# Two-layer graph kernel on one core: the second feed-forward product as seven half-size block products, and a written order for every engine

## The chip, the cores and the metric

The kernel runs on one core of a Trainium2 chip. A core has five engines that run side by side, each with its own instruction queue: TensorE (PE in the profile; its weight loads are listed as PEld), VectorE (DVE), ScalarE (ACT), GpSimd (POOL) and SyncE (SP), which issues the DMAs here. PE reads its operands from the on-chip memory SBUF and writes into the accumulator memory PSUM, which is used in tiles of one bank (128 rows by 512 float32). The metric is the time of one execution in microseconds (us). Before the change the median of three runs is 2792.41 us (2792.07 to 2793.43).

## The reference, cut to what matters

There are 128 graphs of 128 nodes with 256 features, and a 0/1 matrix of edges. Two layers follow each other. The first is a graph-attention layer with a ReLU feed-forward, the second a relational attention with eight heads and a GELU feed-forward. All is float32.

```
# layer 0
h = gat(gat(x, adj, W1, a1), adj, W2, a2)
h = layernorm(x + h)
x = layernorm(h + relu(h @ w_ff1 + b_ff1) @ w_ff2 + b_ff2)
# layer 1
attn = softmax(q @ k.T / sqrt(32));  out = sum over r of (attn * (adj == r)) @ (x @ Wv[r])
x = layernorm(x + out @ Wo + bo)
x = layernorm(x + gelu(x @ W1 + b1) @ W2 + b2)
```

In both feed-forwards the first product takes 256 features to 1024, and the second takes 1024 to 256. The second one is what this change is about.

## The kernel before

The graphs are worked on in 32 groups of four, so a group is 512 tokens (4 x 128). A group passes through five stages: load, gat (two graph-attention steps), ff0 (first feed-forward), att (relational attention) and ff1 (second feed-forward). Each stage is a Python generator that emits instructions and yields a waiting time after each step. `run` is a timetable: it takes the generator whose next time is smallest, lets it emit one step, and puts it back at its time plus the wait. In the main part a group starts every 100 units of the timetable, so that stages of five or six groups interleave. In this order PE and SP are chained by dependencies; the order of DVE, ACT and POOL is left to the scheduler of the framework.

A prefix (function `graph_layers`) loads weights, folds the gains and offsets of the normalisations into the following weights, takes three groups through gat and one through ff0, and scans the whole edge matrix for values above 1. If there are none, as here, the program takes its binary arm, in which only two of the four relations occur; else it takes a general arm. In the first and the last group (`alone`) turned features come from PE transposes (L284); in the others they go out through DRAM and back: DVE turns blocks of 32x32 (L290), SP stores them (zd) and reads them back turned (T, eT).

`feed_forward` (L323) works in two halves.

- First product, already as seven products of blocks (Winograd's form of Strassen's method) in each of two units. A unit owns two 128-row chunks of the lower and two of the upper half of the 1024 hidden features. `moving_sums` forms sums of the token blocks on POOL (L317 to L320), `weight_sums` forms those of the weights once, in the prefix. A unit has four visits, in which `product` (L341) writes into PSUM tiles `chain`, `side` and `p`: three tiles per unit, of seven in the pool `mm`. ACT copies `chain` out between its uses (L347, L354, L359) and `side` (L348), DVE adds (L355, L356), POOL adds the two upper parts (L360), ACT applies the function (L362, L368). The visits alternate between the units.
- Second product, in the plain form. `second` (L386) multiplies, for each of four token blocks, eight chunks fT (128 features by 128 tokens, the stationary operand) with wout (128 by 256, the moving operand): 32 matmuls of 256 columns. Two PSUM tiles hold the result, DVE adds it to the tokens (L396), then `normalised` follows: statistics on DVE (L258, L259), four small steps on POOL (L261 to L265), scaling on ACT (L267). `affine` (L273, POOL) applies gain and offset to the residual.

Other lines that the text below names: L186 folds offsets into wv (chunks of 512 columns), L194 does so for other weights with one moving column; L444, L452, L463 are the products of the gat stage, L478 and L483 those for q and k, L499 the scores (four row groups of 32 side by side), L550 the values, L565 the weighted sum (four column groups), L592 the output product; L512, L514, L515 are the softmax on ACT, DVE and POOL. L408 and L284 are transposes on PE.

Of the kernel before, what the change touches and what calls it, by code (L numbers as in the profile page):

```python
# [24 lines left out]
P = 128  # L25
G = 4
Q = 32
LEAD = 3
FIRST = 1
SCANS = 8  # L30
# [3 lines left out]
    "ff first half": 10, "ff half": 5, "row": 13, "gat": 22, "wh": 5.5,  # L34
# [8 lines left out]
    binary=False, times=TIMES, together=1, period=560, bufs=dict(T=3, tok=2, m=4, mm=6, v=1),  # L43
    begin=dict(load=-97, gat=-61, ff0=48, att=132, ff1=400), early={},
    kept={PE: 0, SP: 0},
# [3 lines left out]
    binary=True, together=2, period=100, bufs=dict(T=5, tok=5, m=2, mm=7, v=2),  # L49
    times=dict(TIMES, **{  # L50
        "sums": 6, "ff visits": (2.5, 2.5, 4, 4, 3.25, 3.25, 3.25, 3.25), "ff first half": 6,
        "ff half": 4, "row": 14.5, "wh": 3.5, "mask": 8.5, "av": 14.5, "wo": 12, "turned": 11,
        "next put": 2.5, "row put": 8, "affine": 13, "store": 21,
    }),
    begin=dict(load=-96, gat=-61, ff0=47, att=129, ff1=303),
    early={
        (-2, "ff1"): -43, (-1, "load"): 5, (0, "att"): -5, (-1, "ff1"): 12, (-2, "att"): -6,
        (-3, "att"): 2, (3, "ff0"): 2, (-4, "ff1"): 5, (4, "ff0"): 2,
    },
    kept={PE: 120, SP: 0},  # L60
)

PREFIX = dict(TIMES, **{
    "sums": 0.5, "ff visits": (1, 1, 2, 1, 0.5, 1, 1, 1), "ff2": 11, "ff first half": 0.5,
    "ff half": 2, "row": 6, "gat": 12.5, "wh": 4.0, "put": 0.5, "lead ff0": 3.5, "scan": 7.5,
    "scans": 25, "gats": (0, 12, 24), "fold": 24.5, "ffs": (48,), "second fold": 31.5,
})
# [16 lines left out]
class Pools:  # L84

    def __init__(self, ctx, tc, bufs):
# [3 lines left out]
        self.ps = ctx.enter_context(tc.tile_pool(name="ps", bufs=bufs["mm"], space=PSUM))  # L90
        self.dr = ctx.enter_context(tc.tile_pool(name="dr", bufs=3, space=bass.MemoryType.DRAM))
# [3 lines left out]
def constants(tc, a, c, cst, tmp, ps):  # L95
# [67 lines left out]

    def others():

        c.wq = wload("wq")
        c.wk = wload("wk")
        c.wv = wload("wv")
        c.bv = cst.tile([P, R * D], F32, name="bv")
        nc.sync.dma_start(c.bv, on_all_rows(11, R))  # L170
        c.wo = wload("wo")
        c.w1 = wload("w1")
        c.w2 = wload("w2")
# [43 lines left out]

def per_row(v, n):

    return v[:, :, None].to_broadcast([P, v.shape[-1], n])  # L220


def stages_of(tc, a, out, c, pools, plan):
# [14 lines left out]
    TB, KB = plan["bufs"]["T"], plan["bufs"]["tok"]  # L238
# [13 lines left out]
    def normalised(y, first=0, n=G):  # L252
# [565 lines left out]
```

## Time and profile before

| | before |
|---|---|
| median of 3 runs | 2792.41 us |
| profiled execution | 2792.19 us, its span 2790.4 us |
| busy PE / weight load | 2714.0 / 2148.0 us |
| busy DVE / ACT / POOL | 1507.7 / 1675.7 / 1569.2 us |
| second product L386, both layers | 913 us, 4096 passes |
| first product L341, all forms | 900 us |
| PE idle from 0 to 156 us | 28 us |
| PE idle from 2700 us to the end | 21 us |
| steady group | 83.3 us |

The profile is one execution, so its parts are to be set against that execution's own time. A group line gives line, engine, operation, written tile <- read tiles, shape and count; then busy time, mean length of one in ns, and the idle time just before with the engine that ended it. A float32 matmul appears as two passes, each with a weight load. In timeline lines the first number is the start and the second the length, both in us; x says how many equal instructions were merged. The length of a matmul includes its way through the array, so the pace of a stream is read from the distance between starts.

### The profile page before, as it was taken

What the parts mean: (1) busy time and instruction counts of PE and PEld (TensorE: products, weight loads), DVE (VectorE), ACT (ScalarE), POOL (GpSimd) and SP (SyncE); (2) the same over time, 40 slices, a digit from 0 to 9 for tenths busy, and PEclk for the clock granted to TensorE, in tenths of its full rate; (3) what the DMA queues carried; (4) which work ended last, traced back from release to release, by engine and by line L of the source; (5) the groups of instructions that cost most, each with busy time, mean ns of one, the idle gap of its engine ahead of it and who ended that gap; (6) DMA issues with size and microseconds to landing.
All of it is one profiled execution on the core that took longest, in us unless ns stands there. A gap on an engine that the chain in (4) does not pass through costs nothing.

```text
span 2790.4 us, 46726 instructions
## 1 busy us (share of the span) xinstructions
PE 2714.0 (97%) x16618; PEld 2148.0 (77%) x16618; DVE 1507.7 (54%) x2882; ACT 1675.7 (60%) x5067; POOL 1569.2 (56%) x1613
## 2 busy tenths in 40 slices
PE   7889999999999999999999999999999999999988
PEld 5667787777788777788777778777778777777767
DVE  5544565555565555565555555555556555556442
ACT  4445565666565666576565666565666566666444
POOL 2334565655665655575565565565566565566453
PEclk8999999999999999999999999999999999999989
DMA  8134555655645655655655655655554565564320
GB/s 304 32 80 96 119 115 122 128 114 123 132 111 114 139 106 119 142 109 109 141 115 112 138 112 113 132 119 113 132 118 112 127 128 112 125 134 91 90 54 16
DMA packets 1136394, 324.04 MB, mean 116 GB/s; under 512 B 886296, under 2 KB 1105944, under 8 KB 1135000
## 3 DMA queue, kind: packets, MB, share of 16 engines
q1 hardware_dynamic: 1136152, 320.96, 51.6%
q8 instruction: 134, 2.20, 0.3%
q14 instruction: 108, 0.88, 0.1%
HBM read 193.35 MB, written 127.52 MB: 115 GB/s over the span
## 4 chain that ended last, share of the span: by engine, by line
PE 73%; ACT 9%; DVE 8%; POOL 6%; issue 3%; DMA 1%; SPq 0%; ACTq 0%; DVEq 0%; POOLq 0%
PE mm L386 31%; PE mm L341 17%; PE mm L550 5%; PE av L565 4%; PE mm L478 4%; PE mm L483 4%; ACT fT L362 2%; PE mm L499 2%; ACT tok L267 2%; PE mm L452 2%; POOL e L515 2%; PE mm L592 2%; DVE nm L503 2%; POOL tok L273 2%; DVE st L258 2%
## 5 line engine op out<-in xcount | busy, mean ns | idle before, releaser
L273 POOL TENSOR_TENSOR tok<-tok,ln_rows 128x512 f32<-128x512 f32 x460 | 624.9, 1375 | 11.8 <-DVE T L290 3.5
L386 PE MATMUL mm<-w,fT 128*128 128x256 f32 x2048 | 465.1, 383 | 0.0
L386 PE MATMUL mm<-wf,fT 128*128 128x256 f32 x2048 | 448.2, 379 | 0.0
L386 PEld LDWEIGHTS mm<-w,fT 128*128 128x128 f32 x2048 | 385.3, 190 | 60.1 <-issue 6.5
L386 PEld LDWEIGHTS mm<-wf,fT 128*128 128x128 f32 x2048 | 389.4, 190 | 53.5 <-ACT fT L368 0.3
L512 ACT ACTIVATE e<-mm,nm 128x128 f32<-128x128 f32 x1024 | 358.4, 401 | 39.7 <-DVE nm L503 35.8
L515 POOL TENSOR_TENSOR e<-e,s 128x1024 f32<-128x1024 f32 x128 | 241.8, 1896 | 246.5 <-DVE s L514 131.8
L317 POOL TENSOR_TENSOR t<-T 128x256 f32<-128x256 f32 x64 | 53.9, 842 | 537.2 <-DMA T<-zd 534.5
L534 DVE TENSOR_TENSOR m<-eT,am 128x1024 f32<-128x1024 f32 x128 | 175.7, 1375 | 332.2 <-DMA eT<-zd 331.9
L267 ACT ACTIVATE tok<-tok,nmr,rstd 128x256 f32<-128x256 f32 x464 | 242.8, 610 | 165.0 <-POOL nmr L265 150.2
L512 ACT ACTIVATION_READ_ACCUMULATOR e<-mm,nm 128x1 f32 x1024 | 247.5, 242 | 0.0
L550 PE MATMUL mm<-wv,T 128*128 128x512 f32 x512 | 234.4, 601 | 0.0
L419 ACT ACTIVATE e<-e,wh 128x128 f32<-128x128 f32 x232 | 74.1, 390 | 228.9 <-DMA e<-zsd 228.9
L360 POOL TENSOR_TENSOR fT<-fT 128x512 f32<-128x512 f32 x128 | 162.1, 1276 | 67.2 <-ACT fT L359 67.2
L341 PE MATMUL mm<-T,w 128*128 128x256 f32 x768 | 192.3, 379 | 1.2 <-ACT fT L354 1.2
L341 PE MATMUL mm<-T,wf 128*128 128x256 f32 x768 | 192.7, 379 | 0.0
L362 ACT ACTIVATE fT<-fT,col 128x512 f32<-128x512 f32 x256 | 170.9, 717 | 26.9 <-DVE fT L356 26.5
L503 DVE TENSOR_REDUCE nm<-mm 128x4 f32<-128x512 f32 x256 | 163.6, 681 | 30.9 <-PE mm L499 30.9
L396 DVE TENSOR_TENSOR tok<-tok,mm 128x512 f32<-128x512 f32 x116 | 79.1, 682 | 177.6 <-PE mm L386 173.8
L258 DVE BATCH_NORM_STATS2 st<-tok 128x6 f32<-128x256 f32 x464 | 173.2, 411 | 3.0
L433 POOL TENSOR_TENSOR e<-e,s 128x512 f32<-128x512 f32 (+1 forms) x70 | 68.0, 972 | 188.9 <-DVE s L432 188.8
L550 PEld LDWEIGHTS mm<-wv,T 128*128 128x128 f32 x512 | 98.9, 194 | 97.7 <-issue 87.1
(141 smaller groups left out, 5198.3 us busy)
## 6 DMA issues: line engine op xcount, KB each, us to landing
zd<-e SPq DMA_DIRECT2D x480, 128.0 KB, 3.5
eT<-zd SPq DMA_DIRECT2D x120, 512.0 KB, 5.2
zd<-T SPq DMA_DIRECT2D x364, 128.0 KB, 3.3
T<-zd SPq DMA_DIRECT2D x91, 512.0 KB, 4.7
xt<-in_xT_dram SPq DMA_DIRECT2D x32, 512.0 KB, 6.4
e<-zsd SPq DMA_DIRECT2D x58, 256.0 KB, 5.7
tok<-in_x_dram SPq DMA_DIRECT2D x29, 512.0 KB, 5.0
out_dram<-tok SPq DMA_DIRECT2D x28, 512.0 KB, 4.7
```

What stands on the lines that cost most here:

```text
L258: nc.vector.bn_stats(st, y[:, b])
L267: nc.scalar.activation(y[:, b], y[:, b], AF.Identity, bias=nmr[:, b:b + 1], scale=rstd[:, b:b + 1])
L273: engine.tensor_tensor(y[:, b:b + n], y[:, b:b + n], v[:, None, :].to_broadcast([P, n, D]), op)
L341: nc.tensor.matmul(p[:, i], win[k][:, ts(f0 + i, P)], hs[k], start=first and i == 0, stop=True, skip_group_check=True)
L360: nc.gpsimd.tensor_add(hi[:, :, 1], hi[:, :, 1], hi[:, :, 0])
L362: nc.scalar.activation(lo[:, i], lo[:, i], func, bias=bin_[:, f0 + i:f0 + i + 1])
L386: nc.tensor.matmul(ys[b // 2][:, b % 2], fT[f][:, ts(b, N)], wout[:, f], start=b % 2 == 0 and n == 0, stop=n == FC - 1, skip_group_check=True)
L503: nc.vector.tensor_reduce(nm.rearrange("p j i -> p (j i)"), p.rearrange("p j i n -> p (j i) n"), AX.X, OP.max, negate=True)
L512: nc.scalar.activation(e[:, k], p[:, j, i], AF.Exp, bias=nms[q][:, j, i:i + 1], accum_out=s[:, k:k + 1])
L515: nc.gpsimd.tensor_mul(e, e, per_row(s, N))
L534: nc.vector.tensor_tensor(m, eT, at[:, b][:, None, :].to_broadcast([P, H, N]), OP.mult)
L550: nc.tensor.matmul(p, hT[:, b, f], wv[:, f, r:r + 2], start=f == 0, stop=f == DC - 1)
```

## The change

- The second product becomes seven products of blocks too. The hidden features are split in lower and upper half, the tokens in two pairs of graphs, the output columns in two halves of 128. `second_sums` forms differences of the weights once in the prefix (four subtractions on DVE for each layer). In each feed-forward `summed` forms, per unit, two sums on DVE and one difference on POOL, and a second POOL subtraction follows when product 2 has read its operand. Each of the seven products is 8 matmuls of 128 moving columns. Two PSUM tiles hold four half-bank results (`chain`, `last`, `side`, `other`), which DVE adds to the tokens in eight additions of 128x256.
- The first product's visits are cut differently: 1 and 2, then 6 and 5, then 7 and 3, then 4, with two PSUM tiles per unit instead of three. In the binary arm the units are visited in the order 0, 0, 1, 0, 1, 0, 1, 1.
- `run` chains every engine. Each step has waits of its own (`steps`, and lists in the prefix), and a table of lags gives every DVE, ACT and POOL instruction of a step a place in its engine's queue: time of the step plus lag.
- Token buffers are five fixed tiles used in turn, where there were three fixed and five in a pool. The statistics tiles of the normalisations have a name per place. The load of xT moves from 96 to 166.75 units before the group's time. The edge scan has 16 pieces in place of 8, into five buffers and two token tiles. Only two relations of wv are loaded and folded in the prefix; the general arm loads the others itself.

The core of the diff:

```diff
-    begin=dict(load=-96, gat=-61, ff0=47, att=129, ff1=303),
+    begin=dict(load=-166.75, gat=-56.45, ff0=40.85, att=130.4, ff1=296.05),
...
+def second_sums(nc, c, w, name):
+    k, half = w.shape[1] // 2, w.shape[2] // 2
+    b11, b12, b21, b22 = w[:, :k, :half], w[:, :k, half:], w[:, k:, :half], w[:, k:, half:]
+    t1, t2, t4 = c.second[name]
+    nc.vector.tensor_sub(t1, b12, b11)
+    nc.vector.tensor_sub(t2, b22, t1)
+    nc.vector.tensor_sub(t4, b21, t2)
+    nc.vector.tensor_sub(b12, b22, b12)
+    return None, b11, b21, b22, t4, t1, t2, b12
...
             product(chain, 1, True)
+            product(side, 2, True)
+            nc.scalar.copy(lo[:, :, 0], chain)
+            nc.vector.tensor_add(lo[:, :, 0], lo[:, :, 0], side)
+            yield
+            product(chain, 6)
             product(side, 5, True)
-            nc.scalar.copy(lo[:, :, 0], chain)
+            nc.scalar.copy(lo[:, :, 1], chain)
             nc.scalar.copy(hi[:, :, 0], side)
             yield
-            p = ps.tile([P, 2, T // 2], F32, name="mm")
-            product(chain, 6)
-            product(p, 2, True)
+            product(chain, 7)
             product(side, 3)
...
+        def summed(u):
+            lo, hi = halves[u]
+            a11, a12, a21, a22 = lo[:, :, 0], hi[:, :, 0], lo[:, :, 1], hi[:, :, 1]
+            s1, s2 = (wk.tile([P, 2, T // 2], F32, name=f"sum{i}") for i in (1, 2))
+            nc.vector.tensor_add(s1, a21, a22)
+            nc.vector.tensor_sub(s2, s1, a11)
+            nc.gpsimd.tensor_sub(a21, a11, a21)
+            return None, a11, a12, a12, a22, s1, s2, a21
...
-                nc.tensor.matmul(ys[b // 2][:, b % 2], fT[f][:, ts(b, N)], wout[:, f],
-                                 start=b % 2 == 0 and n == 0, stop=n == FC - 1, skip_group_check=True)
...
+        first, second = (ps.tile([P, 2, 2, D // 2], F32, name="mm") for _ in range(2))
+        chain, last, side, other = first[:, 0], first[:, 1], second[:, 0], second[:, 1]
+        low, high = (y[:, h:h + 2].rearrange("p b (n d) -> p n b d", n=2) for h in (0, 2))
...
+                        nc.tensor.matmul(p[:, j], parts[u][k][:, i, ts(j, N)], wout[k][:, 2 * u + i],
+                                         start=id(bank) not in done, stop=True, skip_group_check=True)
...
+        parts = [summed(0)]
+        for p, k in (chain, 1), (other, 2), (last, 4):
+            product(p, k, (0,))
+        nc.gpsimd.tensor_sub(parts[0][3], parts[0][3], parts[0][6])
+        yield TIMES["ff first half"]
+        parts.append(summed(1))
+        yield TIMES["ff sums"]
+        product(other, 2, (1,))
+        add(low[:, 0], other)
+        product(chain, 1, (1,))
+        product(last, 4, (1,))
+        nc.gpsimd.tensor_sub(parts[1][3], parts[1][3], parts[1][6])
+        add(low[:, 0], chain)
+        add(high[:, 0], last)
+        yield TIMES["ff 56"]
+        product(side, 5, (0, 1))
+        product(chain, 6, (0, 1))
+        add(high[:, 1], side)
+        add(low[:, 1], chain)
+        yield TIMES["ff 37"]
+        product(side, 3, (0, 1))
+        product(chain, 7, (0, 1))
+        add(low[:, 1], side)
...
+            y = c.y[g % TOKENS]
...
+            if lag is not None:
+                queues.setdefault(i.engine, []).append((t + lag, len(queues.get(i.engine, ())), i))
...
+    for queue in queues.values():
+        queue.sort(key=lambda x: x[:2])
+        for (_, _, first), (_, _, i) in zip(queue, queue[1:]):
+            after(i, first)
```

In the changed kernel's own line numbers, which the prediction uses where it speaks of its queues: L653 is the first product, L659, L664 and L669 ACT's copies of `chain`, L665 that of `side`, L671 POOL's addition of the upper parts, L675 and L679 the function, L687 and L688 the two sums, L689, L720 and L728 POOL's subtractions, L710 the second product, L715 the additions to the tokens, L586 the affine step, L845 the scores, L909 the weighted sum.

## Prediction

> **What bounds the kernel now.** I read first the page's shares of the span, then its 40 slices, then the chain that ended last: each says whether one engine is the end of everything.
>
> ```profile
> PE 2714.0 (97%) x16618; PEld 2148.0 (77%) x16618; DVE 1507.7 (54%) x2882; ACT 1675.7 (60%) x5067; POOL 1569.2 (56%) x1613
> PE   7889999999999999999999999999999999999988
> PEclk8999999999999999999999999999999999999989
> PE 73%; ACT 9%; DVE 8%; POOL 6%; issue 3%; DMA 1%; SPq 0%; ACTq 0%; DVEq 0%; POOLq 0%
> ```
>
> TensorE is busy 97% of the span, at full clock but in the first and last slices. The next view is a table of stretches. One group of four graphs takes 83.3 us: the same instruction (L341, t by w) starts at 1500.23 and at 1583.52. Columns: length, then busy time of PE, weight load, DVE, ACT, POOL, each with its instructions, then clock and DMA.
>
> ```profile
> 1500.20:1583.50 83.30, 82.77 (x512) 65.82 (x513) 46.88 (x88) 52.26 (x159) 49.33 (x51) 1.00 0.56 121
> ```
>
> In the steady part PE idles 0.5 us of 83.3, and no other engine passes 52.3. So time is TensorE time, and what shortens it must shorten PE's own stream. The groups of instructions (columns: form, count, busy, mean ns) say how much of that stream the change touches:
>
> ```profile
> L386 PE MATMUL mm<-w,fT 128*128 128x256 f32 x2048 | 465.1, 383 | 0.0
> L386 PE MATMUL mm<-wf,fT 128*128 128x256 f32 x2048 | 448.2, 379 | 0.0
> L386 PEld LDWEIGHTS mm<-w,fT 128*128 128x128 f32 x2048 | 385.3, 190 | 60.1 <-issue 6.5
> ```
>
> The second product is 913 us, a third of PE. A float32 matmul is recorded as two passes, each with its own weight load, so the 32 matmuls of one feed-forward are 64 passes. The mean of 379 is a latency. The pace is the distance between starts, and the timeline (start, length, instructions) gives it:
>
> ```profile
> 1545.08 13.98 PE L386 MATMUL mm<-wf,fT 128*128 128x256 f32 x64
> 1558.99 0.43 PE L565 MATMUL av<-eT,v 128*32 128x128 f32 x8
> ...
> 129.72 1.91 PE L284 MATMUL mm<-ident,e 128*128 128x128 f32 x16
> 131.46 1.89 PE L341 MATMUL mm<-T,wf 128*128 128x256 f32 x8
> ...
> 77.14 3.63 PE L194 MATMUL mm<-col,w 128*128 128x1 f32 x32
> 80.63 1.93 PE L463 MATMUL mm<-wh,e 128*128 128x256 f32 x5
> ...
> 1508.99 1.17 PE L499 MATMUL mm<-kT,T 32*128 32x128 f32 x32
> 1510.09 7.17 PE L386 MATMUL mm<-w,fT 128*128 128x256 f32 x32
> ```
>
> One block of 64 passes takes 13.91 us, 217 ns a pass. In the second layer the same work stands in three blocks (7.11 + 3.56 + 3.45 = 14.12 us). I take the mean, 14.0 us for each feed-forward, 64 of them.
>
> **The change, part by part.**
>
> *Seven products of half size.* Each product is 256 tokens by 512 by 128, so 8 matmuls with 128 moving columns; seven are 56 matmuls, 112 passes instead of 64. What is streamed falls from 64 x 256 to 112 x 128 columns, by an eighth, but the weight loads grow by three quarters. All hangs on the pace of a 128-column pass whose weights are new each time; before has no such row. The nearest rows bound it. The 16 transposes (128 columns, new weights, load 141 ns instead of 190) pace 1.74 / 16 = 109 ns. L194 (one column, full 190 ns loads) paces 3.49 / 32 = 109 ns: so a stream of full loads alone needs no more than that. L499 has both, 186 ns loads and 128 columns, but in four row groups side by side: 1.10 / 32 x 4 = 137 ns with the switch of shape included. The range is 109 to 137 ns. I take 109: the load row and the column row give it separately, and a 217 ns pass hides its 190 ns load today. Then 112 x 0.109 = 12.2, and 0.1 for the switches of shape, 12.3 us. Saved: 1.7 x 64 = **-109 us**. At 137 ns it is 15.4 + 0.1, so +96 us; from 125 ns (14.0 / 112) the change loses.
>
> The Trainium skill, "TensorE: Matmul & The Clock Gate", section "Back-to-back issue gap", speaks against this: in a stream of weight load and matmul pairs it gives about 81 ns for 128 columns where columns alone give 56, because the load is part of the spacing. If our 109 grew in that ratio, an estimate from that page, a pass would take 158 ns, a feed-forward 17.7 us, and about 235 us would be added where I count 109 saved. The two rows of 109 ns speak otherwise, but neither has full loads and full columns at once.
>
> *New additions.* Per feed-forward DVE gets four sums of 128x512 (0.69 us, as L356) and eight additions of half size (0.42, as the 128x256 sum L664) for two of 0.68: +2.8 + 3.4 - 1.4 = 4.8 us. POOL gets four subtractions of 128x512 (1.28, as L360): 5.1 us.
>
> ```profile
> L356 DVE TENSOR_TENSOR fT<-fT,mm 128x512 f32<-128x512 f32 x128 | 87.7, 685 | 78.3 <-ACT fT L354 64.7 <-PE mm L341 12.7 <-PE mm L452 0.9
> L360 POOL TENSOR_TENSOR fT<-fT 128x512 f32<-128x512 f32 x128 | 162.1, 1276 | 67.2 <-ACT fT L359 67.2
> L273 POOL TENSOR_TENSOR tok<-tok,ln_rows 128x512 f32<-128x512 f32 x460 | 624.9, 1375 | 11.8 <-DVE T L290 3.5
> ```
>
> Per group DVE goes from 46.9 to 56.5 and POOL from 49.3 to 59.5 us of some 80; ACT stays at 52. None becomes the bound, and the work lies beside PE: 0 us on the path, as long as the order lets it.
>
> *The written order.* Every engine now has a fixed order. In the first layer's feed-forward the second product follows the last visit of unit 1 at once. Count from the end of unit 0's last product on PE: unit 1's last two visits end at 2.6 us, unit 0's products 1, 2, 4 at 5.2, then unit 1's product 2 until 6.1 and product 1. On ACT stand from 0.95: copy 0.58, 0.47, 0.72, 0.50, 0.47 x 2, 0.50, 0.47, 0.50, and last the two 128x512 activations of unit 1 (0.72 each, L362), which product 1 reads: they end at 6.3 and 7.1. PE wants the first at 6.1 and the second at 6.9 and gets them with 0.2 us of signalling: 0.7 us lost in all, 31 times: **+22 us**. Below, nothing (ACT earlier); above, 2 us a group, as PE's worst wait for ACT's L359 in before (2.1). The second layer has L824, L829, scores and the weighted sum between (9 us of PE) and loses nothing. The 0.5 us that PE waited for L359 per group may go or stay; I count it as staying. What is queued behind such a wait is PE's whole stream.
>
> Product 3 reads POOL's subtraction L728. POOL's order there is L671 twice, L720, an affine, L689, two affines, L689, L728. From L720's start at 4.3 us (product 2 of unit 0 read) that is 4 x 1.28 + 3 x 1.375 = 9.2, so 13.5; PE wants it at 15.2 (7.8, the weighted sum and scores 3.0, products 5 and 6 3.5, half of 3). Margin 1.7 us, cost 0.
>
> *Two PSUM banks instead of three in the first product.* The same 56 passes and the same copies: 0. The second product's two banks are held longer, but six of seven tiles are then in use: 0; above, 0.4 us a feed-forward, one addition late.
>
> *Loads, tokens.* The load of xT now stands earlier on SP and waits there for the last reader of the single buffer; behind it wait the stores and reads of the turned features, which PE needs 10 us later or more. With five token buffers for eight, a group's input is fetched 25 of the timetable's 100 units after the output before it in that buffer is stored. 0; above, 1 us a group.
>
> *Head.* L186 loses a chunk of 512 (4 passes of 0.43): **-1.7**. The four weight differences per layer and 16 scans for 8 add 7 us to DVE, which is busy 61 of the first 100: 0. In group 0's attention, scores are now followed at once by the transposes of e, which need DVE 0.68, 8 x 0.64 of ACT and POOL 1.9, and the second half 5 us more; before had L341 of the next group there. Some of it comes back, because before idles 4.9 us from 157 to 168 and 2.4 from 180 to 200. I lay both orders side by side up to the second L478: **+4** (-4 to +9).
>
> *Tail.* Before mixes the last two groups to 2767 and idles 11.5 us for the softmax and little else before its end. Now the last feed-forward stands alone: wait for the last normalisation and its transposes 4, for POOL's first sums 0.6, for ACT 2, for the activations and s2 2.5: **+9** (0 to +15).
>
> Sum: -109 - 1.7 + 22 + 4 + 9 = -76. The profiled execution took 2792.19 us (span 2790.4), the median of the runs is 2792.41, the same within 0.01%. **Forecast 2716 us.**
>
> **Rivals.**
>
> *Loads do not hide (slower).* Place: every pass of the second product. Price at L499's 137 ns: +96 instead of -109, so 2921 us; it decides from 125 ns. For it: a load's own 190 ns are longer than the pace wanted, so each must overlap its neighbours and the columns too. Against: two rows at 109.
>
> *The written order stalls PE.* Place: product 3 behind POOL's queue, or the visits behind ACT's copies. If POOL comes one softmax multiplication (L515, 1.90) and one affine late, 3.3 - 1.7 = 1.6 us per feed-forward, 60 times, +96: 2812. If it is one affine late on ACT's side only, about half: 2765. For it: just-in-time margins of 1.7 us. Against: POOL and DVE idle 20 us per group.
>
> *Everything hides.* No wait in the first layer, head and tail as before: 2792 - 109 - 2 = 2681; with before's L359 waits gone too, 2670.
>
> *It does nothing on balance:* pace about 119 ns with my waits, 2792 +/- 5.
>
> **How the numbers follow.** Forecast, with its waits somewhat smaller or larger (2690 to 2745): 70%. Everything hides: 8%. Order stalls: 12% (8 faster, 1 same, 3 slower). Loads do not hide: 8%. Nothing: 2%. A difference of 0.2% (5.6 us) is about what a measurement of this kernel can tell from none. Faster 70 + 8 + 8 = 86%, same 1 + 2 = 3%, slower 8 + 3 = 11%. The range 2670 to 2775 leaves out the slow rival, half of the stalls and a bit of the rest.
>
> **What would show it.** Right: 7168 passes of 128x128 in the second product, blocks of 32 in 3.5 us; a group in about 81 us with PE over 98% busy; a first-layer wait of PE on the 128x512 activation near 0.7 us; POOL near 60 us a group. Wrong: blocks of 32 over 4.0 us (loads); PE idle over 2 us a group behind POOL L720 or L728 or ACT (order); head longer by more than 9 us or tail by more than 15.

## The result, and the profile after

Over five runs each, the changed kernel takes 2805.19 us (2800.63 to 2805.93) and the kernel before 2792.41 us. The ratio is 1.0043, with a 95% interval of 1.0028 to 1.0057: slower, where 2716 was forecast. The profiled execution of the changed kernel took 2805.93 us, its span is 2804.1.

The same lines of the page as before: shares, PE's slices, the clock, and the chain that ended last.

```profile
PE 2672.2 (95%) x19686; PEld 2191.4 (78%) x19686; DVE 1910.5 (68%) x3537; ACT 1673.9 (60%) x5067; POOL 1992.6 (71%) x1869
PE   6789999999999999999999999999999999999987
PEclk8889999999999999999999999999999999999998
PE 81%; DVE 12%; ACT 3%; POOL 3%; issue 2%; DMA 0%; SPq 0%; POOLq 0%; ACTq 0%; DVEq 0%
```

PE has 42 us less to do, but its share fell from 97% to 95%. DVE got 403 us more and POOL 423. DVE's part of the chain went from 8% to 12%. The clock is 1.00 in the middle part, as before; in the first 200 us it is lower (second and third digit). The table of stretches (length, then busy time of PE, weight load, DVE, ACT, POOL, clock, DMA), for one group:

```profile
1500.00:1582.55 82.55, 81.25 (x609) 66.88 (x608) 58.59 (x109) 52.14 (x159) 62.44 (x59) 1.00 0.54 122
```

DVE and POOL are near the 56.5 and 59.5 us that were counted, each below 63 of 82.6. Yet PE now idles 1.3 us a group. The second product in the groups of instructions:

```profile
L710 PE MATMUL mm<-wf,fT 128*128 128x128 f32 x2048 | 253.8, 279 | 30.4 <-DVE y L715 29.9
L710 PEld LDWEIGHTS mm<-wf,fT 128*128 128x128 f32 x2048 | 243.3, 193 | 40.1 <-POOL fT L728 30.2
L710 PE MATMUL mm<-w,fT 128*128 128x128 f32 x2048 | 252.5, 278 | 0.5 <-ACT fT L679 0.5
```

The last column is new: in the first layer (wf) PE waits for DVE's additions L715, and its loads' wait is put down to POOL's subtraction L728; in the second (w) there is next to nothing (0.5 us by the last row). The timeline of PE, first the second layer, then the first:

```profile
1532.16 3.74 PE L710 MATMUL mm<-w2s,sum 128*128 128x128 f32 x32
1535.73 3.91 PE L710 MATMUL mm<-w,fT 128*128 128x128 f32 x32
1539.48 1.89 PE L936 MATMUL mm<-wo,oT 128*128 128x256 f32 x8
...
1567.66 2.05 PE L710 MATMUL mm<-wf2s,sum 128*128 128x128 f32 x16
1570.09 2.05 PE L710 MATMUL mm<-wf2s,sum 128*128 128x128 f32 x16 [0.38 <-DVE y L715]
1573.06 3.81 PE L710 MATMUL mm<-wf,fT 128*128 128x128 f32 x32 [0.92 <-DVE y L715]
```

Undisturbed, 32 passes take 3.57 us: 111.6 ns a pass. In the first layer products 5 and 6 (16 passes each) take 2.43 and 2.97 us from start to start instead of 1.8. What DVE does meanwhile:

```profile
1565.55 0.41 DVE L715 TENSOR_TENSOR y<-y,mm 128x256 f32<-128x256 f32 x1
1565.88 1.43 DVE L772 SCALAR_TENSOR_TENSOR e<-e 128x512 f32<-128x512 f32 x1
1567.34 1.65 DVE L773 SCALAR_TENSOR_TENSOR e<-cap,e 128x512 f32<-128x512 f32 x1
1569.02 0.69 DVE L774 TENSOR_REDUCE nm<-e 128x4 f32<-128x512 f32 x1
1569.63 0.41 DVE L715 TENSOR_TENSOR y<-y,mm 128x256 f32<-128x256 f32 x1
1569.95 1.88 DVE L849 TENSOR_REDUCE nm<-mm 128x4 f32<-128x512 f32 x3
1571.83 0.18 DVE L778 RECIPROCAL s<-s 128x4 f32<-128x4 f32 x1
1571.93 0.66 DVE L849 TENSOR_REDUCE nm<-mm 128x4 f32<-128x512 f32 x1
1572.50 0.74 DVE L715 TENSOR_TENSOR y<-y,mm 128x256 f32<-128x256 f32 x2
```

Product 6 starts 0.05 us after the L715 that ends at 1570.04, product 3 0.15 us after the first of the two from 1572.50 on, which ends at 1572.91. The first of these additions reads `last`, the other half of the bank in which product 6 goes on adding to `chain`; the second reads `side`, to which product 3 adds. The written order has put the graph attention's softmax (L772 to L774) and the scores' maxima (L849) ahead of them. POOL's L728, which the second half of product 3 reads, is hardly earlier:

```profile
1566.72 3.40 POOL L586 TENSOR_TENSOR y<-y,ln_rows 128x512 f32<-128x512 f32 x2
1570.08 1.27 POOL L689 TENSOR_TENSOR fT<-fT 128x512 f32<-128x512 f32 x1
1571.31 1.26 POOL L728 TENSOR_TENSOR fT<-fT,sum 128x512 f32<-128x512 f32 x1
```

**Where the time went.** I cut the span at the first q product (L478, now L824) of group 1 and of the last group. Up to group 1: 174.7 us before, 196.1 after, +21.4. The 30 groups between: 2489.0 and 2476.4, -12.6. From the last one to the end: 126.7 and 131.6, +4.9. Together +13.7, the difference of the spans. Forecast were +2 for the head, -81 for the 30 groups (3.4 less pace, 0.7 more wait each) and +9 for the tail; the remaining -6 of the sum falls to the feed-forwards outside these groups. So the loop failed by 68 us, and the head by 19.

### The profile page after: what moved, and what is told of

Its sections match the earlier page's. It is cut to its first block, busy times and chain, and to the rows that moved or that the text cites. A ratio compares the mean times of both kernels' runs of the same rounds, so it can differ in the third digit from the quotient of the medians.

```text
span 2804.1 us, 54277 instructions
## 1 busy us (share of the span) xinstructions
PE 2672.2 (95%) x19686; PEld 2191.4 (78%) x19686; DVE 1910.5 (68%) x3537; ACT 1673.9 (60%) x5067; POOL 1992.6 (71%) x1869
## 4 chain that ended last, share of the span: by engine, by line
PE 81%; DVE 12%; ACT 3%; POOL 3%; issue 2%; DMA 0%; SPq 0%; POOLq 0%; ACTq 0%; DVEq 0%
PE mm L653 27%; PE mm L710 23%; PE mm L895 7%; PE mm L824 4%; PE mm L790 4%; PE mm L829 4%; PE mm L936 4%; DVE nm L849 3%; PE av L909 2%; PE mm L798 2%; PE mm L809 2%; DVE e L773 2%; DVE y L715 2%; DVE e L772 1%; PE mm L845 1%
## 5 line engine op out<-in xcount | busy, mean ns | idle before, releaser
L586 POOL TENSOR_TENSOR y<-y,ln_rows 128x512 f32<-128x512 f32 x508 | 720.0, 1432 | 197.1 <-DVE T L603 184.0
L580 ACT ACTIVATE y<-y,nmr,rstd 128x256 f32<-128x256 f32 x512 | 273.2, 594 | 312.7 <-POOL nmr L578 282.3
L858 ACT ACTIVATE e<-mm,nm 128x128 f32<-128x128 f32 x1024 | 366.8, 390 | 86.3 <-DVE nm L849 83.8
L861 POOL TENSOR_TENSOR e<-e,s 128x1024 f32<-128x1024 f32 x128 | 254.0, 1985 | 84.4 <-DVE s L860 84.4
L715 DVE TENSOR_TENSOR y<-y,mm 128x256 f32<-128x256 f32 x512 | 203.5, 409 | 137.1 <-PE mm L710 136.6
L671 POOL TENSOR_TENSOR fT<-fT 128x512 f32<-128x512 f32 x128 | 214.8, 1678 | 103.1 <-ACT fT L669 103.1
L710 PE MATMUL mm<-wf,fT 128*128 128x128 f32 x2048 | 253.8, 279 | 30.4 <-DVE y L715 29.9
L710 PEld LDWEIGHTS mm<-wf,fT 128*128 128x128 f32 x2048 | 243.3, 193 | 40.1 <-POOL fT L728 30.2
L710 PEld LDWEIGHTS mm<-w,fT 128*128 128x128 f32 x2048 | 240.7, 192 | 24.0 <-issue 19.8
L710 PE MATMUL mm<-w,fT 128*128 128x128 f32 x2048 | 252.5, 278 | 0.5 <-ACT fT L679 0.5
L687 DVE TENSOR_TENSOR sum<-fT 128x512 f32<-128x512 f32 x128 | 113.4, 886 | 184.6 <-issue 96.2
L858 ACT ACTIVATION_READ_ACCUMULATOR e<-mm,nm 128x1 f32 x1024 | 235.6, 230 | 0.0
L720 POOL TENSOR_TENSOR fT<-fT,sum 128x512 f32<-128x512 f32 x64 | 83.4, 1303 | 212.0 <-PE av L909 129.5
L571 DVE BATCH_NORM_STATS2 st<-y 128x6 f32<-128x256 f32 x512 | 198.5, 408 | 2.3
L689 POOL TENSOR_TENSOR fT<-fT 128x512 f32<-128x512 f32 x128 | 190.5, 1499 | 9.2 <-DVE sum L687 9.2
L679 ACT ACTIVATE fT<-mm,col 128x256 f32<-128x256 f32 x256 | 120.1, 473 | 120.5 <-POOL fT L671 120.2
L603 DVE STREAM_TRANSPOSE e<-e 128x1024 f32<-128x1024 f32 x120 | 148.2, 1235 | 62.4 <-POOL e L861 62.2
L653 PE MATMUL mm<-T,wf 128*128 128x256 f32 x768 | 187.3, 382 | 0.0
L675 ACT ACTIVATE fT<-fT,col 128x512 f32<-128x512 f32 x256 | 182.0, 725 | 3.0 <-DVE fT L670 2.6
```

The costliest lines, as they stand in the source:

```text
L571: nc.vector.bn_stats(st, y[:, b])
L580: nc.scalar.activation(y[:, b], y[:, b], AF.Identity, bias=nmr[:, b:b + 1], scale=rstd[:, b:b + 1])
L586: engine.tensor_tensor(y[:, b:b + n], y[:, b:b + n], v[:, None, :].to_broadcast([P, n, D]), op)
L653: nc.tensor.matmul(p[:, i], win[k][:, ts(f0 + i, P)], hs[k], start=first and i == 0, stop=True, skip_group_check=True)
L671: nc.gpsimd.tensor_add(hi[:, :, 1], hi[:, :, 1], hi[:, :, 0])
L689: nc.gpsimd.tensor_sub(a21, a11, a21)
```

## The experiments

The table holds all runs. Period, PE's time by product, PE's idle time, and DVE's and POOL's busy time are us per group, means over 16 groups in the middle of the trace. PE's time is counted from each pass to the start of the next, less the idle time before that.

| kernel | median us | ratio to before, 95% | period | second product | first product | PE idle | DVE | POOL |
|---|---|---|---|---|---|---|---|---|
| before | 2792.4 | 1 | 83.08 | 28.02 | 24.51 | 0.31 | 46.3 | 49.2 |
| after | 2805.2 | 1.0028-1.0057 | 82.56 | 26.28 | 24.80 | 1.34 | 58.4 | 62.4 |
| e1 | 2806.6 | 1.0037-1.0065 | 82.80 | 26.09 | 24.91 | 1.20 | 58.1 | 62.5 |
| e2 | 2803.3 | 1.0027-1.0054 | 82.56 | 26.28 | 24.80 | 1.33 | 58.5 | 62.4 |
| e3 | 2809.9 | 1.0047-1.0074 | 82.84 | 25.83 | 24.88 | 1.56 | 58.1 | 62.5 |
| e4 | 2811.8 | 1.0054-1.0082 | 82.54 | 26.27 | 24.81 | 1.31 | 58.5 | 62.4 |
| e5 | 2918.1 | 1.0432-1.0461 | 86.57 | 28.02 | 24.93 | 3.32 | 45.8 | 49.8 |
| e6 | 2728.1 | 0.9757-0.9784 | 80.31 | 25.58 | 24.58 | 0.00 | 49.0 | 49.8 |
| e7 | 2830.4 | 1.0123-1.0154 | 83.78 | 25.95 | 24.81 | 1.55 | 64.9 | 58.2 |
| e8 | 2826.5 | 1.0106-1.0137 | 83.46 | 26.39 | 24.61 | 1.85 | 64.0 | 58.0 |
| e9 | 2807.7 | 1.0034-1.0062 | 82.76 | 26.11 | 24.87 | 1.62 | 58.7 | 62.0 |
| e10 | 2740.3 | 0.9803-0.9830 | 80.50 | 25.78 | 24.59 | 0.00 | 57.0 | 51.9 |
| e11 | 2761.7 | 0.9873-0.9903 | 81.47 | 25.83 | 24.59 | 0.92 | 51.1 | 60.5 |
| e12 | 2879.4 | 1.0294-1.0323 | 85.39 | 26.28 | 25.19 | 3.78 | 61.1 | 55.1 |
| e13 | 2836.4 | 1.0139-1.0166 | 83.22 | 25.58 | 24.66 | 2.39 | 62.9 | 51.9 |
| e14 | 2851.4 | 1.0188-1.0216 | 83.81 | 25.93 | 24.66 | 2.63 | 61.2 | 57.9 |
| e15 | 3253.5 | 1.1632-1.1668 | 97.87 | 27.55 | 27.69 | 12.42 | 57.5 | 60.3 |
| e16 | 2758.4 | 0.9869-0.9899 | 81.06 | 25.76 | 24.74 | 0.24 | 59.7 | 62.0 |
| e17 | 2835.9 | 1.0146-1.0174 | 83.05 | 25.84 | 24.69 | 1.93 | 65.1 | 52.3 |
| e18 | 2795.1 | 0.9992-1.0010 | 82.33 | 26.24 | 24.61 | 1.33 | 59.7 | 61.0 |

### e1 to e3: the order in the first feed-forward

The rows of the first layer's lag table. e1 has the second and third line's V values, e2 the G values, e3 both.

```
-V 102.1 103.3 | G 104.9
-V 101 103.5 105.7 | G 105.3
-V 93.5 94.5
+V 102.1 103.3 | G 102.3
+V 101 103.5 103.6 | G 101.8
+V 90.5 91.3
```

> The changed kernel with three numbers of the steady groups' lag table changed: in the first feed-forward DVE adds the product called last before the three operations of the graph attention's softmax (L772 to L774) instead of behind them, and the sums of products 5 and 6 before and between the maxima L849 instead of behind all four. POOL's order stays. Theory (PE waits in every first feed-forward for two things at once, DVE's additions L715 and POOL's subtraction L728, which end at 1573.0 and 1572.6 us in the profile): the wait before product 6 goes, but product 3 starts only when POOL is through, about 0.4 us sooner in each of 30 groups: 2805 - 12 = about 2793 us. Rival 1 (DVE's order alone is the fault): product 3 starts 1.8 us sooner, 2750 us. Rival 2 (the missing time is PE's own pace): 2805 us, no change.

> The changed kernel with two numbers of the lag table changed: in the first feed-forward POOL does the second unit's two subtractions (L689, L728) ahead of the two affine halves L586 of the other stage (3.4 us in the profile) instead of behind them. DVE's order stays. Theory (both queues bind): product 3 still waits for DVE's addition that ends at 1573.0 us, so nothing is gained: 2805 us, within 5. Rival 1 (POOL's queue alone is the fault, as one case of the prediction had it): 1.8 us sooner per group, 2750 us. Rival 2 (PE's own pace): 2805 us as well.

> Both changes of order at once. Theory (both queues bind): product 6 follows product 5 and product 3 follows product 6 without a gap, 1.8 us less in each of 30 groups: 2805 - 54 = about 2750 us. Rival (what PE wins here it waits for later, since DVE and POOL are the chain): 2790 to 2805 us. If PE's own pace were all that is missing: 2805 us.

Theory was that both queues bind. In e1, 0.24 us of the 1.3 us of waiting are left, in the middle of product 3, 0.05 us behind the end of L728; in e2 all of it is left. Neither is faster: e2's 2803 us was its theory's, and also its second rival's; e1's 2807 us was not, since PE now waits 0.8 us a group at the scores for ACT's L830. e3's trace bears the theory out at the place itself: products 5, 6, 3 and 7 follow each other without a gap, and the second product falls by 0.45 us. But nothing was gained in time, which was the rival's case, with 2810 us even above its range: PE's idle time rose to 1.56 us. The chain of waits of e3, from the window of one group (start, length, what), shows where it went:

```profile
1510.34 1.26 DVE T L603
1511.60 0.07 issue
1511.67 4.71 POOL y L586 x3
1516.38 1.22 POOL fT L671
1517.60 4.13 POOL y L586 x3
1521.73 2.22 POOL fT L671
...
1526.40 0.59 ACT kT L830
1526.98 0.04 issue
1527.03 0.95 PE mm L845 x24
```

Twelve microseconds of POOL in a row, and behind it ACT and then PE's scores. POOL has 30% of e3's chain, against 3% in the changed kernel. The theory had the place right, but not that a second loop of waits stood just as close.

### e4: the stretch ahead of the branch, ordered by the scheduler

```
 PREFIX: lags={ (0, 0): ..., (3, 0): ... }
+PREFIX: lags={}
```

> The changed kernel without the lag table of the stretch ahead of the branch: there DVE, ACT and POOL are ordered by the scheduler again, PE and SP stay in the written order; the loop of the groups is untouched. Theory (the head is 11 us longer since DVE got 7 us more to do there and its written order holds the first graph attentions and the first feed-forward back): some of it comes back, 2795 us, and the transposes of group 0's y (L597) come at about 105 instead of 115 us. Rival 1 (DVE is simply full there, in any order): 2800 to 2810 us. Rival 2 (the written order is the better one): over 2815 us.

2811.8 us, between the two rivals, and group 0's first q product at 123.0 us instead of 119.2 (107.9 before). The theory falls: the written order is no worse than the scheduler's. In the chain of the changed kernel DVE stands from 90.8 to 102.3 us with L810, folded weights, a scan and sums, where before PE's second product stood. What each of them costs there was not separated; without the sums of hidden values (e6) it is 113.8, without those of the weights (e5) 115.5, but in e2, which leaves nothing out and has the changed kernel's order on every engine up to 400 us, 112.0. So these differences are no larger than those between executions.

### e5: the plain second product in the changed kernel's order

```
-parts = [summed(0)]
-for p, k in (chain, 1), (other, 2), (last, 4):
-    product(p, k, (0,))
...
+for b in range(G):
+    second(b, order[:FC // 2])
...
+for k in (0, 2):
+    nc.vector.tensor_add(y[:, k:k + 2], y[:, k:k + 2], ys[k // 2])
```

> The changed kernel with the second product as it was before (64 passes of 256 columns into two banks, two 128x512 additions, untransformed weights), and with all else of the change: the written order, the first product with two banks, the five token buffers, the shorter scan chunks. The places in the written order of what fell away are simply dropped. Theory (the seven block products do save PE time in the loop, 26.28 instead of 28.02 us a group by PE's steps from pass to pass, but only half of what was predicted, and 1.0 us of it goes in new waits): the loop is 0.7 us a group slower here, +22, and the head 6 us shorter since DVE is spared the eight sums of weights: 2805 + 22 - 6 = about 2820 us. Rival 1 (the written order and the longer head are what costs, the seven products gain 2.5 us a group): 2880 us. Rival 2 (the seven products are a loss as such): 2775 us.

2918 us, above all cases. PE's time for the second product is that of before, 28.02, but PE idles 3.3 us a group behind ACT's copies and POOL's L632, at places that have nothing to do with the second product. The order was laid out for other lengths, so this run says nothing about the product itself. It does show how much a fixed order loses when what it orders changes.

### e6, e9, e10, e11: the sums left out, or computed for nothing

```
-nc.vector.tensor_add(s1, a21, a22)          # e6, e11: L687, L688 out
-nc.vector.tensor_sub(s2, s1, a11)
-nc.gpsimd.tensor_sub(a21, a11, a21)         # e6, e10: L689, L720, L728 out
-nc.gpsimd.tensor_sub(parts[u][3], parts[u][3], parts[u][6])
+return None, a11, a12, a12, a22, a22, a21, a21    # e6; e9 too, with all sums kept
```

> The changed kernel without the sums and differences of the hidden values that the seven products need (L687 to L689, L720, L728: eight operations of DVE and eight of POOL a group left out, so that the products run on the wrong blocks); the products and their additions stay. Theory (PE's own pace is 111.7 ns a pass plus about 0.1 us at each start of a block, so that 25.7 us a group is the floor of the second product, and the waits of the first feed-forward come from queues that these operations fill): idle time of PE 0.3 us a group, period 81.2 us, 2805 - 42 = about 2760 us. Rival 1 (DVE's and POOL's extra work costs nothing, the order of the queues does): 2800 us. Rival 2 (PE's pace is slowed by what DVE and POOL do beside it): under 110 ns a pass, 2745 us or less.

> The changed kernel with all sums and differences of the hidden values still computed (L687 to L689, L720, L728 at their places in the queues), but into tiles that no product reads; the products run on the raw blocks, so PE never waits for a sum (the output is not the layers'). Theory (what costs is the time that these operations take in DVE's and POOL's queues, where PE waits for the additions L715 that stand behind them): period near 82 us, 2790 to 2805 us. Rival (PE waits for the sums themselves): as without them, period 80.3 us, 2728 us.

> The changed kernel with DVE's sums (L687, L688) and without POOL's four subtractions per feed-forward (L689, L720, L728 left out; products 3, 4 and 7 run on wrong blocks). Theory (DVE and POOL lengthen each other when both work from SBUF to SBUF: L773 takes 0.69 us alone and 1.64 us beside a POOL operation, L772 0.65 and 1.43; so POOL's eight operations a group reach PE through DVE's queue, which is up to 3 us shorter in the first feed-forward without them): the wait before products 6 and 3 goes, period 80.4 us, 2735 us. Rival (only DVE's own extra operations count): 82 us, 2790 us.

> The other half left out: POOL's subtractions stay, DVE's two sums per unit (L687, L688) go (products 3 to 6 run on wrong blocks). Theory (DVE's queue between products 2 and 3 of the first feed-forward is 4.5 us shorter, by L687 and L688 there): period 80.5 us, 2735 us. Rival (POOL's queue sets the period as soon as DVE's is short, as in e3_both_orders): 82 us or more, 2790 us.

These four settle where the loss is. Without the sums, one group of e6 reads

```profile
1500.00:1580.30 80.30, 80.30 (x609) 66.78 (x608) 48.90 (x101) 52.12 (x160) 49.82 (x51) 1.00 0.55 124
```

PE is busy every microsecond, and the time is 2728, 65 us better than before and below what its theory had (2760). Rival 2's time came (2745 or less), but not for its reason: within a block the passes start 111.6 ns apart, as in the changed kernel. With the sums computed but not used (e9) it is 2808, as in the changed kernel: the rival, that PE waits for the sums themselves, falls. What costs, in this order, is the time that these operations hold DVE and POOL. POOL's eight alone are worth 65 us (e10), DVE's eight alone 44 (e11), both together 77: each half is more than half of it. e10 came out as its theory had it, e11 between its theory (2735) and its rival (2790). In e11 the only wait left is the one for L715, 0.92 us a group, and the softmax tells why. The groups of instructions of the changed kernel, then of e10, where the same lines are called L770 and L769, over the same 1200 us (busy, mean ns):

```profile
L773 DVE SCALAR_TENSOR_TENSOR e<-cap,e 128x512 f32<-128x512 f32 x28 | 32.7, 1168 | 0.5
L772 DVE SCALAR_TENSOR_TENSOR e<-e 128x512 f32<-128x512 f32 x28 | 29.2, 1041 | 0.0
```

```profile
L770 DVE SCALAR_TENSOR_TENSOR e<-cap,e 128x512 f32<-128x512 f32 x30 | 20.8, 692 | 0.5
L769 DVE SCALAR_TENSOR_TENSOR e<-e 128x512 f32<-128x512 f32 x30 | 20.6, 686 | 5.1 <-ACT e L762 5.1
```

In the changed kernel half of the L773 take 0.69 us and half, those of the first feed-forward, 1.65: they start while a POOL operation is running. In e11 it is again half of them at 1.64. In e10, without POOL's subtractions, POOL is through by then and all take 0.69. So POOL's work reaches PE through DVE's queue: softmax longer by 1.7 us, L715 later by as much.

### e7, e8, e12: work taken from POOL and given to DVE

```
-affine(y, "12", b, 2, nc.vector if last else nc.gpsimd)        # e7 (with e3's order), e8
+affine(y, "12", b, 2, nc.vector)
-nc.scalar.copy(hi[:, :, 1], chain)                             # e12
-nc.gpsimd.tensor_add(hi[:, :, 1], hi[:, :, 1], hi[:, :, 0])
+nc.vector.tensor_add(hi[:, :, 1], hi[:, :, 0], chain)
```

> Both changes of order of the run before (e3_both_orders), and the four operations L586 that scale the output are done by DVE instead of POOL, in a place of its written order where it was idle for 3.9 us (5.6 us less for POOL, 2.8 us more for DVE a group). Theory (with the waits of the first feed-forward gone POOL's queue sets the period: the chain of e3_both_orders runs through POOL for 30% of its time, six L586 and two L671 in a row): period 81.4 us instead of 82.8, about 2765 us. Rival 1 (another queue is as close behind, ACT's or DVE's): 2795 to 2805 us. Rival 2 (DVE becomes the bound): over 2810 us.

> The changed kernel with the output's four operations L586 on DVE as in e7_affine_dve, but with its own order in the first feed-forward. Theory (there the chain of a group runs PE, then DVE from L715 to the last L715, and not POOL): period 82.5 us as in the changed kernel, 2805 us within 6. Rival (POOL's load is what slows DVE and PE there, by contention or by its queue): 81.5 us, 2770 us.

> The changed kernel, with the correct output, where the last block of the first product is made by one DVE addition from PSUM (chain plus the copy of side, 0.68 us by L670) instead of ACT's copy L669 and POOL's addition L671 (1.68 us each): four operations of POOL (6.7 us) and four of ACT (2 us) a group less, four of DVE (2.7 us) more. Theory (POOL's and DVE's operations from SBUF to SBUF lengthen each other, and POOL's share of that falls): period 81.5 to 82 us, about 2785 us. Rival 1 (DVE's queue is what PE waits for, in any case, and it gets longer): 83.5 us, 2835 us. Rival 2 (no change in sum): 2800 to 2810 us.

The theory falls in e7: the time is rival 2's (over 2810), but with DVE busy 65 of 83.8 us its load is not the bound, and PE waits 1.0 us a group at the scores for ACT's L675. e8 and e12 lost more than any case had expected. In e7 and e8 the price was wrong: on DVE the L586 took 1.51 us each (mean of 60), not 0.7, since all of them ran beside POOL operations. That is 6 us more for DVE a group, and the chain of e7 runs through it. The same holds for e8 (1.44 us each, DVE 64.0). In e12 the additions took the 0.68 us expected, but PE waited up to 2.1 us for them: the bank that product 4 goes on adding into is now freed by DVE's queue instead of by ACT's. For L715 it waited 1.7 us a group besides.

### e13, e14, e17: POOL's subtractions on DVE

```
-nc.gpsimd.tensor_sub(a21, a11, a21)                            # e13, e17
+nc.vector.tensor_sub(a21, a11, a21)
-nc.gpsimd.tensor_sub(parts[u][3], parts[u][3], parts[u][6])    # e13, e14, e17
+nc.vector.tensor_sub(parts[u][3], parts[u][3], parts[u][6])
```

> The changed kernel, with the correct output, where POOL's eight subtractions a group (L689, L720, L728) are made by DVE, in places of its written order that lie ahead of the products that need them and where it was idle or could wait (the additions of the first feed-forward ahead of the softmax as in e3_both_orders, the mask's L785 0.06 periods later). Theory (the price of the sums is their time in the queues and what DVE and POOL lose to each other, and on DVE a subtraction takes 0.69 us instead of 1.3 to 1.5 us): DVE 57.0 + 8 x 0.69 = 62.5 us and POOL 52 us a group, PE as without POOL's subtractions, period 80.5 to 81 us, 2740 to 2755 us, faster than before. Rival (DVE's queue in the first feed-forward is full, whatever POOL does): 82.5 us or more, 2800 us and up.

> As e13_subs_dve, but only the four subtractions that come last (L720, L728) are moved to DVE; L689 stays on POOL. Theory (as above, by half): POOL 57 us, DVE 61 us a group; L689 still lengthens the softmax's L772 and L773, so PE waits 0.3 to 0.9 us a group: period 81 to 81.5 us, 2755 to 2775 us. Rival (POOL's queue is no matter): like e13_subs_dve, within 5 us.

> Correct output: e13_subs_dve (POOL's subtractions on DVE) with POOL's order repaired in the same way: the two additions L671 ahead of the L586 before them, and the output's four L586 together in the 8.4 us in which POOL stood idle before L779. Theory (POOL has 52 us of work a group, its written order alone held the others up): PE's idle time falls from 2.4 to under 0.5 us, period 81 us, 2765 us with the longer head of e13_subs_dve. Rival (each repair uncovers the next wait): period 82.5 us or more, 2815 us and up.

The theory falls in all three: period 83.1 to 83.8. The rivals had the times of e13 and e17 right, but e13's not the place, as the first feed-forward holds e13 up no more; e14's rival falls as well (15 us above e13). DVE and POOL have the busy times expected (62.9 and 51.9 in e13), and PE does not wait in the second product, but it idles 2.4 us a group, 1.6 of them behind ACT's L659 and 0.8 behind ACT's L830. In the window of one group the chain of e13 runs through POOL's L586 and L671 (28%), and before them are 8.4 us in which POOL waits for nothing that the profile shows, so its place in the order is the likely cause. In e17, where that is repaired, the chain passes DVE's sums, L772 to L774 and L849, then ACT's L858 and POOL's L861 to L578. Ten microseconds a group less for POOL were no help. That it is DVE's 61 to 65 us that undo it fits e17's chain, but no run shows it alone.

### e15: the loop ordered by the scheduler

```
 BINARY: lags={ "gat": ..., "ff1 -1": ... }
+BINARY: lags={}
```

> The changed kernel without the lag tables of the loop: DVE, ACT and POOL are ordered by the scheduler as before the change, PE and SP stay in the written order of the changed kernel. It tells whether the written order, a part of the change of its own, costs or saves. Theory (the written order was laid out for these very operations; what costs is their work): no better, 2805 us or more, up to 2900. Rival (the written order puts the additions of the first feed-forward behind the softmax for no need, and the scheduler does not): 2770 us or less.

3253 us, 350 more than even the theory's upper end, and PE idle 12.4 us a group. With PE's order kept as it is, the written order of the other engines saves 450 us over the scheduler's. It is no cost as a whole, only at single places.

### e16 and e18: mending POOL's order, with and without e3

The second layer's lag table; e16 is e3 with these four values, e18 has them alone.

```
-V 93.1 | S 98.3 | G 94.1
+V 93.1 | S 98.3 | G 92.8
-V 87.1 | S 91.1 | G 91.8
+V 87.1 | S 91.1 | G 83.3
-G 62.2 70.5
-G 48.2 57.7
+G 62.2 91.1
+G 48.2 75.95
```

> Correct output, all the work of the changed kernel: e3_both_orders with four more places of POOL's written order changed, read from the chain of waits of e3_both_orders. The two additions L671 of the second feed-forward go ahead of the three affine halves L586 that stand before each of them, and two of the output's four L586 go behind the normalisation of the next group, where POOL was idle for 3.5 us. Theory (the load of POOL and DVE can be hidden, it only stands in the wrong places: 62.5 and 58 us of work against 81): PE's idle time falls from 1.6 to under 0.5 us a group, period 81.5 us, 2765 us. Rival (with queues as full as this each repair uncovers the next wait): period 82.4 us or more, 2795 us and up.

> Correct output: the changed kernel with the four places of POOL's order alone that e16_pool_order_2 added (L671 ahead of the L586 before it, two of the output's L586 later), without the order of the first feed-forward from e3_both_orders. Theory (PE waits at two places of a group, one after the other in DVE's first feed-forward and in POOL's second, and each alone holds the period; so neither repair helps without the other): the wait for L715 in the first feed-forward stays, 1.3 us a group, period 82.4 us, 2800 us. Rival (POOL's places were the whole of it): as e16_pool_order_2, 81.1 us, 2760 us.

e16 takes 2758.4 us, 0.9884 of before (0.9869 to 0.9899) and the fastest kernel here that computes all. Its group:

```profile
1500.00:1581.05 81.05, 80.89 (x610) 66.66 (x609) 59.80 (x109) 52.05 (x159) 62.01 (x58) 1.00 0.55 123
```

It does the same work as the changed kernel, on the same engines, with POOL at 62 and DVE at 60 us, and PE idles 0.2 us. Of the 2.25 us a group that the changed kernel lies above e6, 0.75 are left. Half of the L773 take 1.64 us here too, so the longer softmax costs only where an operation that PE wants stands behind it. e18 has a period of 82.33 and still waits 1.3 us a group for L715; it and e16 came out as their theories had it. The four cases: neither repair 2805, the first 2810, the second 2795, both 2758. Two loops of waits held the period, each at about 82.5 us, and opening one only shows the other.

## Why the prediction was wrong

- **New additions: wrong, and this is the step that failed.** "None becomes the bound, and the work lies beside PE: 0 us on the path, as long as the order lets it." The amounts were nearly right (56.5 and 59.5 us counted, 58.4 and 62.4 measured), and none is the bound. But the order did not let it: e6 against the changed kernel puts the price at 79 us of span, 67 of them in the 30 groups. I had judged by busy share, where the question was when each queue gets to the operation that PE waits for. e16, with the same work, shows that two thirds of the loss in the loop are the order's.
- **A wait put at 0.** The eight half-size additions L715 were priced at 0.42 us each. They also read PSUM banks that PE goes on writing, so PE's products wait for DVE in mid-feed-forward. The prediction has this only as the upper end of a term of 0, "0.4 us a feed-forward, one addition late". Before, DVE's additions came only at the end of the second product. This wait is 1.3 us a group in the changed kernel, all of it in the first layer's feed-forward.
- **Durations under load.** I took 0.69 and 1.28 us from rows of a kernel in which DVE and POOL met less. In the changed kernel L687 takes 0.89 on average, L689 1.50, L671 1.68 (1.28 as L360 before), L586 1.43. From L720's start to L728's end 10.45 us pass in the window shown, where 9.2 were counted. L720 also starts 1.2 us later than counted, at 1562.12: it waits for DVE's sum L688, which the prediction's count left out. So the margin of 1.7 us for L728 was gone: it ends at 1572.57, and an undisturbed PE would reach the second half of product 3, which reads it, at about 1572.1. L728 is 0.4 us late, DVE's addition 1.7 us.
- **Pace: right in kind, mis-sized.** Counted 109 ns a pass and 12.3 us a feed-forward, saving 1.7. Measured 111.7 ns within a block, and about 0.14 us more for each of the four blocks of a group (25.58 - 224 x 0.1117 = 0.56 in e6); without waits 25.58 / 2 = 12.8 us, saving 1.2. That is 0.5 x 64 = 32 us less. The rival that loads do not hide falls: 112 ns is far from 125.
- **The Trainium skill's rule**, "TensorE: Matmul & The Clock Gate", section "Back-to-back issue gap", had stood against the change. By its ratio of 81 to 56, an estimate, a pass would have taken 158 ns. The measured 111.7 ns decide: full loads of 192 ns and 128 columns cost little more than either alone here.
- **The ACT wait of 0.7 us: wrong, +22 counted, about nothing found.** PE itself never waits for L675, the activation meant, and 1.0 us in the whole span for L679. In e6's steady groups nothing is left, nor is before's 0.3 us for L359. This offsets the pace: the 30 groups of e6 are 80 us shorter, where 81 was forecast, and that they agree so well is luck.
- **Rival "order stalls": the nearest.** It had its place at product 3, and POOL's queue as the smaller of the two things that product 3 waits for. It had not DVE's, and 12% was too little for it. Its price was 1.6 us in both feed-forwards, 96 us; measured are 67 us in the 30 groups, with PE waiting in the first feed-forward alone, 1.3 us a group, where its sign asked for over 2. That its 2812 us lie close to 2805 is partly luck: pace and head make up for the rest.
- **Head: mis-sized.** +2 counted, +21 measured at group 1. DVE's 7 us more were put at 0 since it was busy 61 of the first 100 us. But after the change it is busy 17 to 19 of each 20 us from 40 to 100, and the chain runs through it. PE's granted clock is 0.85 and 0.82 in the first and second 100 us, against 0.86 and 0.91 before. Without the sums (e6) group 1 starts 6 us earlier, at 189.7, but so it does in e2, at 190.3, with the changed kernel's own order up to there and a clock of 0.90 in the first 100 us. So the head is 16 to 21 us longer, depending on the execution, and what the sums cost in it, and what the clock does, stays open.
- **Tail:** +9 counted, +5 measured.

## What to carry to other kernels

An operation on an engine with a low share is free only if its place in that engine's queue comes before the consumer wants it; so count, for each wait of the bounding engine, what stands ahead of the releaser in its queue, and remember that PSUM additions between accumulating products are such waits. Removing one wait tells little when several loops of waits have nearly the same period: look at the chain after each repair and mend the next place before judging. Leaving work out, and computing it into tiles that nobody reads, are two cheap runs that separate "too much work" from "waits for the result".

## What the runs showed of the hardware

- DVE and POOL lengthen each other, here by 0.4 to 1.0 us an instruction. In the changed kernel an L586 of POOL runs from 1566.72 to 1568.44; DVE's L773 starts at 1567.34 and ends at 1568.99, 1.65 us, and the next L586, started at 1568.39, takes 1.73 instead of 1.27. Where L773 starts first (1540.39), it takes 0.69, and the L861 that starts at 1540.55 takes 2.29 instead of 1.89. DVE's L774 and L715, with one input or with PSUM, keep 0.69 and 0.41 us beside POOL. The Trainium skill, "SBUF — State Buffer", section "SBUF: two separate sides", says that whichever of a GpSimd operation and a DVE operation with two SBUF inputs starts first holds the shared ports for the whole instruction; these rows agree.
- A pause of PE costs more than its idle time: before the waits of 0.38 and 0.92 us the last pass counts with its whole length of 275 ns instead of the 112 to the next start, and the first pass after them takes 184 to 213, some 0.25 us in addition for each wait. In e3, without the waits, the second product is 0.45 us a group shorter.
